# Cross-attention beside self-attention cells: where the weights are divided by their sum, how far their transposes follow the scores, and the number of places for parts

## The chip, the cores and the metric

The kernel runs on one core of a Trainium2 chip. The metric is the device time of one execution in microseconds (us); less is better. A core has five engines that run their own instruction streams in order and wait for one another through semaphores: TensorE (PE, matrix products; its weight loads are listed as PEld), VectorE (DVE), ScalarE (ACT), GpSimd (POOL) and SyncE (SP, which issues most of the DMA transfers). Tiles lie in SBUF; PE writes its results to the eight banks of PSUM, each 128 partitions by 512 float32 numbers.

## The reference

A chain of two transformer blocks over x of 2 batches x 1024 tokens x 256 features, all in float32. Each block has self-attention (16 heads of 16 features, 1024 keys), cross-attention to a context of 64 rows per batch, and a feed-forward part. In block 0 the feed-forward part is a mixture: a router picks two of eight experts for each token. In block 1 it is one dense network, and the cross-attention's scores get a bias of -10000 where the mask is 0. Cut to the cross-attention, which is what the change touches:

```python
def layer_norm(x, w, b):
    mu = jnp.mean(x, axis=-1, keepdims=True)
    var = jnp.mean(jnp.square(x - mu), axis=-1, keepdims=True)
    return (x - mu) * jax.lax.rsqrt(var + EPS) * w + b
...
xn = layer_norm(x, ln1_w, ln1_b)
q = _heads(xn @ q_w.T)                  # 16 heads of 16
k = _heads(codebook_embeds @ k_w.T)     # 64 keys per batch
v = _heads(codebook_embeds @ v_w.T)
attn = jnp.einsum('bhnd,bhmd->bhnm', q, k) * SCALE
bias = (1.0 - codebook_mask.astype(attn.dtype))[:, None, None, :] * -10000.0
attn = jax.nn.softmax(attn + bias, axis=-1)
ca = _merge(jnp.einsum('bhnm,bhmd->bhnd', attn, v)) @ ca_proj_w.T
x = x + ca
```

Block 0 does the same without the bias, with biases on the projections.

## The kernel before

**One order for four engines.** The whole program is one function, and the order of the instructions on PE, DVE, ACT and SP is the order in which the Python code issues them; only POOL's is left to a scheduler. Around the change this order comes from two things: a loop over cells, and a stream of tasks that fills the cells.

**Cells.** Self-attention of a block is cut into 16 passes (2 batches x 2 halves of the queries x 4 groups of four heads), each of 8 cells (blocks of 128 keys), so 128 cells per block; `for cell in range(ncell + 2)` (L959) runs over them. A cell has, in this order on PE: four score matmuls with keys on partitions (`score` of kind "b", L816), interleaved with four score matmuls for the cell ten ahead (kind "a", L805; `LEAD = 10`), from which DVE takes row maxima out of PSUM (L812); ACT takes exponentials of the four "b" banks into SBUF (L822). Every second cell `product` (L858) multiplies the exponentials of two cells by the values (L867, eight matmuls into one bank). Its first result of a pass is copied by ACT to `acc` (L876), each later one to a tile `part` (L879), which is then added to `acc` (L880). Two places are allotted for `part`. The addition is on the engine that `helper()` names: POOL as long as maxima are still to be taken (`maxima[0]`), DVE in the last ten cells of a block. A cell that has only this is called bare.

**The stream.** Everything else of a block is cut into tasks, Python generators that issue some instructions and then yield: a positive number is the declared cost of what was issued, a number of zero or below is a wait, which puts the task's next step at least one cell later, and more cells for a longer wait (in units of `CELL = 2.9`). In every cell the loop takes steps from the tasks that are able to run until their declared cost reaches a rate, 2.5 a cell in block 0 and 1.1 in block 1 (more where tasks have a due cell). What is left when the cells are over is run behind them by `Stream.rest`, in the order of rank; that stretch is called the tail of a block. A bank is taken from the list `free` and put back when the code that drains it has been issued, so a later user of the bank waits on chip for the one that drains it.

**Cross-attention.** It is worked in four units a block, each of 512 queries (`cross_tasks`, L1076, in both blocks). A unit is three tasks one behind the other: `norm` (layer norm and transposes to features on partitions), `weigh` (L1103) and `share` (L1273, the output projection, L437 and L445). A unit starts its norm when the one before it is "weighed". `weigh` makes the queries q_c (L1113, L1120) and then works in two groups g of eight heads; a group has four tiles r of two heads each, 128 queries on partitions by 4 blocks of queries x 2 heads x 64 keys:

- scores of two tiles (L1143; in block 1 the mask's bias is put into the bank by matmuls first, L1134), copied by ACT to sc_c in SBUF (L1154);
- `largest`: a maximum over the 64 keys on DVE (L1163), subtracted by POOL in place (L1164); in the tail both are on DVE and read PSUM;
- `weights_turned`: four 128x128 transposes per tile on PE (L1179), then the exponential on ACT from PSUM to pt_c (L1183);
- `product`: four matmuls by the values (L1192), copied by ACT over q_c (L1209); and the sums of the exponentials by 16 matmuls with columns of ones and zeros out of `picks` (L1202), whose reciprocals DVE takes as one 128x128 tile (L1211);
- `divided`: four matmuls spread the reciprocals over the heads' rows (L1217), and DVE multiplies q_c by them (L1224). For the second group this stands at the start of `share`.

A unit that begins while maxima are being taken follows a list of 11 steps, mostly one step a cell; in the tail it follows another list of the same steps with shorter waits.

**Mixture, block 0.** Behind each unit's `share` stands its dispatch (`dispatch_task`, L1306): router (L1332), ranks by a matmul (L1392), and the scattering of the rows to their experts by POOL's indirect DMAs (L1429). The experts' tiles (`expert_tiles`, L1442) load sorted rows through SP (L1570), transpose them (L1622) and run the two layers of each expert (L1656, L1686). Block 1's feed-forward part is `forward_task` (L1816, L1828).

**Other users of what the change touches.** `side_by_side` (L756 to L782) closes the last self-attention heads of block 0 and has a reciprocal tile `inv` of its own. `picks` is a constant of 768 columns loaded once; O_SUM, O_HEAD, O_ROWS and O_PART are the column offsets of its parts. The tag "xn" has six places of 128x256 for centred rows (L357) in the pool `small`.

## Time and profile before

| what | us |
|---|---|
| three runs | 1624.6, 1626.58, 1629.66; median 1626.58 |
| the profiled execution | 1611.58 |
| its span, first to last instruction | 1609.8 |
| mean granted TensorE clock in it | 0.988 |

The same execution by stretches, cut at whole microseconds near the first score of a cell (busy time of each engine, us, as the profile's windows give it):

| stretch | length | PE | DVE | ACT | POOL | clock |
|---|---|---|---|---|---|---|
| 0 to 52, before the first cells | 52 | 42.0 | 34.2 | 14.3 | 16.0 | 0.97 |
| 52 to 254, cells 0 to 51 of block 0 | 202 | 200.6 | 150.5 | 145.4 | 64.3 | 0.95 |
| 254 to 583, cells 52 to 127 with cross-attention | 329 | 323.8 | 240.3 | 224.0 | 109.8 | 0.98 |
| 583 to 943, tail of block 0 | 360 | 354.3 | 147.2 | 125.4 | 68.1 | 1.00 |
| 943 to 1175, cells 0 to 60 of block 1 | 232 | 229.7 | 170.3 | 170.3 | 67.5 | 1.00 |
| 1175 to 1446, cells 61 to 127 with cross-attention | 271 | 266.6 | 192.6 | 188.7 | 74.4 | 1.00 |
| 1446 to 1610, tail of block 1 | 164 | 157.9 | 47.6 | 46.7 | 10.9 | 1.00 |

How to read the profile's lines: a group of instructions gives its line in the kernel, its engine, the operation, what is written and read by the tiles' names, partitions x elements, how many there are, then busy time in us and the mean ns of one, then the idle time of the engine just before them and what ended most of it. Matmuls are pipelined, so the time of one matmul from start to end is longer than the distance from its start to the start of the one behind it; the busy time of a group of matmuls counts such overlaps once. A line of the timeline gives the start, the duration, the engine and the line, and in brackets the wait ahead of it and who ended it.

### The profile page before, as it was taken

Reading aid. Unit: us, or ns where it says so; the run is one execution under the profiler, and the core shown is the slowest. Engines: PE = TensorE matmul, PEld = TensorE weight load, DVE = VectorE, ACT = ScalarE, POOL = GpSimd, SP = SyncE. Lnnn points to the kernel's source line nnn. Section 1 sums busy time; section 2 is a strip of 40 time slices with the busy share of each in tenths; the row PEclk is TensorE's granted clock in tenths of the full one; section 3 lists DMA queues with packets and bytes.
Section 4 is the critical chain, followed back from the end, with each engine's and each line's share of the span. In section 5 each row is a group of like instructions: output and inputs, shape, how many; then the busy total and the mean of one; then the engine's idle time right before and its main releaser. Section 6 shows DMA issues by size and latency. Waiting matters only on the chain. (4 is left out here: it accounts for less than half of the span.)

```text
span 1609.8 us, 28322 instructions
## 1 busy us (share of the span) xinstructions
PE 1574.8 (98%) x10710; PEld 876.0 (54%) x10710; DVE 982.6 (61%) x2094; ACT 914.7 (57%) x1770; POOL 410.9 (26%) x546
## 2 busy tenths in 40 slices
PE   7999999999999999999999999999999999999998
PEld 3433444444544447888888653344344445446766
DVE  5797766677679747511114458876777777854400
ACT  3487767666765665332223337876776676674321
POOL 2233423135235203311112033411222322311000
PEclk9899999999999999999999999999999999999999
DMA  5334311101000115386556320101010002000000
GB/s 158 114 134 169 138 27 31 28 25 47 15 21 34 54 50 196 105 278 205 187 188 216 92 78 23 35 21 24 31 38 17 22 14 84 20 9 21 14 13 26
DMA packets 55751, 121.07 MB, mean 75 GB/s; under 512 B 12218, under 2 KB 26428, under 8 KB 55228
## 3 DMA queue, kind: packets, MB, share of 16 engines
q1 hardware_dynamic: 51772, 109.07, 20.9%
q0 software_dynamic: 3456, 9.51, 1.6%
q8 instruction: 86, 1.41, 0.4%
q10 hardware_dynamic: 384, 0.66, 0.2%
q14 instruction: 53, 0.43, 0.1%
HBM read 71.68 MB, written 38.88 MB: 69 GB/s over the span
## 5 line engine op out<-in xcount | busy, mean ns | idle before, releaser
L812 DVE TENSOR_REDUCE mx_s<-banks 128x1 f32<-128x512 f32 x1024 | 634.0, 681 | 209.5 <-PE banks L805 207.2
L822 ACT ACTIVATE pt_s<-banks 128x512 f32<-128x512 f32 x1024 | 532.8, 609 | 157.1 <-PE banks L805 123.8
L805 PE MATMUL banks<-KS,QS 16*128 16x512 f32 x2048 | 535.1, 631 | 2.9 <-DVE count L1446 1.4
L816 PE MATMUL banks<-qb_s,KS 32*128 32x512 f32 x2048 | 516.8, 622 | 6.9 <-DVE qb_s L715 3.6
L880 POOL TENSOR_TENSOR acc_s<-acc_s,part_s 128x512 f32<-128x512 f32 x141 | 179.4, 1272 | 434.5 <-ACT part_s L879 433.9
L816 PEld LDWEIGHTS banks<-qb_s,KS 32*128 32x128 f32 x2048 | 180.8, 187 | 178.7 <-DVE mx_s L812 106.3
L867 PE MATMUL banks<-pt_s,v_s 128*20 128x512 f32 x2048 | 262.7, 604 | 1.5 <-DVE mx_s L812 1.0
L805 PEld LDWEIGHTS banks<-KS,QS 16*128 16x128 f32 x2048 | 200.3, 186 | 71.7 <-issue 34.2
L867 PEld LDWEIGHTS banks<-pt_s,v_s 128*20 128x20 f32 x2048 | 43.1, 98 | 185.8 <-ACT pt_s L822 130.4
L1686 PE MATMUL banks<-w_slot,h_s 128*128 128x256 f32 x640 | 143.1, 380 | 0.0
L1686 PEld LDWEIGHTS banks<-w_slot,h_s 128*128 128x128 f32 x640 | 120.6, 190 | 19.7 <-DVE mx_s L812 1.5
L879 ACT COPY part_s<-banks 128x512 f32<-128x512 f32 x155 | 92.7, 598 | 62.3 <-PE banks L867 52.6
L1695 DVE SCALAR_TENSOR_TENSOR ys<-banks,gate,b 128x256 f32<-128x256 f32 x40 | 19.3, 482 | 163.0 <-PE banks L1686 161.8
L1662 ACT ACTIVATE h_s<-banks,w_slot 128x256 f32<-128x256 f32 x104 | 43.7, 471 | 111.1 <-issue 64.0
L1656 PE MATMUL banks<-xsT,w_slot 128*128 128x256 f32 x416 | 95.4, 381 | 0.7 <-ACT xsT L376 0.7
L1701 POOL DMA_INDIRECT results<-ys,to x40 | 38.8, 970 | 223.0 <-DVE ys L1695 180.5
L1656 PEld LDWEIGHTS banks<-xsT,w_slot 128*128 128x128 f32 x416 | 77.4, 190 | 14.9 <-DVE mx_s L812 2.3
L1164 POOL TENSOR_TENSOR sc_c<-sc_c,mx_c 128x512 f32<-128x512 f32 x38 | 40.0, 1053 | 97.6 <-DVE mx_c L1163 97.5
L1819 ACT ACTIVATE h_f<-banks,w_ff 128x512 f32<-128x512 f32 x32 | 22.0, 687 | 73.9 <-PE banks L1816 73.9
L635 PE MATMUL banks<-xT_s,w_att 128*128 128x512 f32 x128 | 63.9, 635 | 0.0
L1828 PE MATMUL banks<-w_ff,h_f 128*128 128x256 f32 x256 | 57.3, 380 | 0.0
L1662 ACT ACTIVATE h_s<-banks,spare 128x256 f32<-128x256 f32 x56 | 23.4, 471 | 58.7 <-issue 30.4
(272 smaller groups left out, 1640.2 us busy)
## 6 DMA issues: line engine op xcount, KB each, us to landing
w_slot<-in_ff_w_dram SPq DMA_DIRECT2D x40, 576.0 KB
sorted_rows<-fill SPq DMA_DIRECT2D x36, 520.0 KB
w_slot<-in_ff_w_dram SPq DMA_DIRECT2D x26, 514.0 KB
whole<-acc_s SPq DMA_DIRECT2D x30, 256.0 KB
spare<-in_ff_w_dram SPq DMA_DIRECT2D x14, 514.0 KB
xs<-sorted_rows SPq DMA_DIRECT2D x20, 260.0 KB
y<-results SPq DMA_DIRECT2D x16, 256.0 KB
QS<-stq_s SPq DMA_DIRECT2D x124, 32.0 KB
```

What stands on the lines that cost most here:

```text
L635: nc.tensor.matmul(p, lhsT=w[:, at + k * D + pair * P : at + k * D + (pair + 1) * P], rhs=xT[b][:, k, blk * 512 : (blk + 1) * 512], start= ...
L805: nc.tensor.matmul(sc, lhsT=QS[h % 4][r, qc * P : (qc + 1) * P], rhs=K[r, kh * 512 : (kh + 1) * 512], start=True, stop=True,)
L812: return i, lambda: nc.vector.tensor_reduce(mx[h][:, qc, j, kh : kh + 1], sc, AX.X, ALU.max)
L816: nc.tensor.matmul(sc, lhsT=K[r, n * P : (n + 1) * P], rhs=QB[h][r, :], start=True, stop=True)
L822: nc.scalar.activation(pt, sc, AF.Exp, scale=SCALE)
L867: nc.tensor.matmul(o[32 * j : 32 * j + VW, :], lhsT=V[b][:, cell % 8, 4 * g + j, :], rhs=exps.pop((cell, j)), start=(cell == cells[0]), st ...
L879: nc.scalar.copy(part, o)
L880: helper().tensor_tensor(acc[h], acc[h], part, ALU.add)
L1656: nc.tensor.matmul(ph[:, n, :], lhsT=w[:, at : at + P], rhs=xT[:, k, :], start=(k == 0), stop=(k == 1),)
L1662: nc.scalar.activation(h1[:, f, :], ph[:, n, :], AF.Gelu, bias=w[:, W_B1 + f : W_B1 + f + 1])
L1686: nc.tensor.matmul(py, lhsT=h1[:, f, h * P : (h + 1) * P], rhs=w[:, f * D : (f + 1) * D], start=(f == 0), stop=(f == 7),)
L1828: nc.tensor.matmul(py[:, n, :], lhsT=h1[:, f, t * P : (t + 1) * P], rhs=w2[:, f * D : (f + 1) * D], start=(f == 0), stop=(f == 7),)
```

## The change

For units that begin while maxima are being taken (`whole`), the weights are now finished with queries on partitions, ahead of the transposes:

- after the subtraction ACT takes the exponential in SBUF in place (`exponentials`), DVE sums over the 64 keys and takes the reciprocals of the eight sums per partition, and `helper()` multiplies the tile by them (`divided`);
- `weights_turned` then transposes finished weights, and ACT only copies them out of PSUM;
- `product` has only the four matmuls by the values and ACT's copy; the sums by matmul, the spreading of reciprocals and the multiplication of q_c are left out, in `share` too.

Such a unit follows a schedule over 19 cells: tile k (0 to 7) has its scores and its subtraction in cell k + 4g (scores for two tiles together), the exponential two cells later, sum and division three cells later; the transposes of two tiles stand seven cells behind their scores, and the products of the groups in cells 11 and 18. Between the cells of this schedule the task yields 0.0 while maxima are being taken and -1.5 afterwards.

A unit that begins in the tail keeps the old steps, renamed `undivided` and `division`, with the masks of ones read from 32 columns that are shifted by 2r in place of four sets of 32. Three further edits: `picks` shrinks from 768 to 680 columns, with its parts moved; the tiles of reciprocals lie in the "xn" places and not in tags of their own; and `part` has three places instead of two.

```diff
@@ -104,10 +104,11 @@
 NCOL = 139
 
 
-O_SUM, O_HEAD = 0, 128
-O_ROWS, O_PART = 640, 704
-NPICK = 768
+O_SUM, O_HEAD = 512, 0
+O_ROWS, O_PART = 552, 616
+NPICK = 680
 
 W_O, W_V, W_Q, W_K = 0, 512, 1024, 1536
 NSELF = 2048
@@ -766,7 +767,7 @@
                         start=(half == 0),
                         stop=(half == 1),
                     )
-            inv = small.tile([P, P], F32, tag="inv", name=f"inv_{names}", bufs=1)
+            inv = small.tile([P, D], F32, tag="xn", name=f"inv_{names}", bufs=6)[:, :P]
             nc.vector.reciprocal(inv, s[:, :P])
             nc.scalar.copy(dst, o)
             free.extend((j, i))
@@ -875,7 +876,7 @@
                 acc[h] = opool.tile([P, 512], F32, tag="acc", name=f"acc_{names}{h}")
                 nc.scalar.copy(acc[h], o)
             else:
-                part = opool.tile([P, 512], F32, tag="part", name=f"part_{names}{cells[0]}")
+                part = opool.tile([P, 512], F32, tag="part", name=f"part_{names}{cells[0]}", bufs=3)
                 nc.scalar.copy(part, o)
                 helper().tensor_tensor(acc[h], acc[h], part, ALU.add)
             free.append(n)
@@ -1125,11 +1126,15 @@
         shape = [P, 4 * 2, SK]
         less, pts, whole_scores = {}, {}, set()
 
+        whole = maxima[0]
         def scores(g, n):
 
             got = [(r, *bank()) for r in (2 * n, 2 * n + 1)]
+            masked = layer == 1
             for t in range(4):
-                for r, _, p in got if layer == 1 else ():
+                for r, _, p in got if masked else ():
                     at = slice(32 * r, 32 * r + 1)
                     nc.tensor.matmul(
                         p[:, t * P : (t + 1) * P].rearrange("p (u k) -> p u k", k=SK),
@@ -1144,7 +1149,7 @@
                         p[:, t * P : (t + 1) * P],
                         lhsT=q[rows, g, t * P : (t + 1) * P],
                         rhs=kbd[rows, g, b].rearrange("p u k -> p (u k)"),
-                        start=(layer == 0),
+                        start=not masked,
                         stop=True,
                     )
             for r, i, p in got:
@@ -1169,6 +1174,17 @@
         def largest(g, r):
             if (g, r) in whole_scores:
                 subtract(less[g, r], less[g, r], nc.gpsimd, f"{g}{r}")
+        def exponentials(g, r):
+            nc.scalar.activation(less[g, r], less[g, r], AF.Exp, scale=SCALE)
+        def divided(g, r):
+            sc = less[g, r].rearrange("p (c k) -> p c k", k=SK)
+            sm = pool.tile([P, 8], F32, tag="smc", name=f"sm_{name}{g}{r}", bufs=4)
+            nc.vector.tensor_reduce(sm, sc, AX.X, ALU.add)
+            nc.vector.reciprocal(sm, sm)
+            helper().tensor_tensor(sc, sc, sm.unsqueeze(2).to_broadcast(shape), ALU.mult)
 
         def weights_turned(g, n):
 
@@ -1180,13 +1196,14 @@
                         p[:, t * P : (t + 1) * P], sc[:, t * P : (t + 1) * P], ident
                     )
                 pt = pts[g, r] = pool.tile([P, 512], F32, tag="p1", name=f"pt_{name}{g}{r}", bufs=4)
-                nc.scalar.activation(pt, p, AF.Exp, scale=SCALE)
+                if whole:
+                    nc.scalar.copy(pt, p)
+                else:
+                    nc.scalar.activation(pt, p, AF.Exp, scale=SCALE)
                 free.append(i)
 
-        inverse = {}
         def product(g):
             i, o = bank()
             for r in range(4):
                 nc.tensor.matmul(
@@ -1196,22 +1213,37 @@
                     start=True,
                     stop=True,
                 )
+            nc.scalar.copy(q[:, g, :], o)
+            free.append(i)
+        inverse = {}
+        def undivided(g):
+            i, o = bank()
+            for r in range(4):
+                nc.tensor.matmul(
+                    o[32 * r : 32 * (r + 1), :],
+                    lhsT=vbd[:, b, 4 * g + r, :],
+                    rhs=pts[g, r],
+                    start=True,
+                    stop=True,
+                )
             j, s = bank()
             for r in range(4):
                 for c in range(4):
                     nc.tensor.matmul(
                         s[32 * c : 32 * (c + 1), :P],
-                        lhsT=picks[:, O_SUM + 32 * r : O_SUM + 32 * (r + 1)],
+                        lhsT=picks[:, O_SUM + 6 - 2 * r : O_SUM + 38 - 2 * r],
                         rhs=pts[g, r][:, c * P : (c + 1) * P],
                         start=(r == 0),
                         stop=(r == 3),
                     )
             nc.scalar.copy(q[:, g, :], o)
-            inv = inverse[g] = pool.tile([P, P], F32, tag="inv", name=f"inv_{name}{g}", bufs=2)
+            inv = inverse[g] = small.tile([P, D], F32, tag="xn", name=f"inv_{name}{g}", bufs=6)[:, :P]
             nc.vector.reciprocal(inv, s[:, :P])
             free.extend((i, j))
 
-        def divided(g):
+        def division(g):
             i, p = bank()
             for c in range(4):
                 nc.tensor.matmul(
@@ -1224,33 +1256,36 @@
             nc.vector.tensor_tensor(q[:, g, :], q[:, g, :], p, ALU.mult)
             free.append(i)
 
-        held.update(ot=q, divided=divided)
-        cost = 1.9 if layer else 1.0
-        SC, LA, TU, PR, DI = scores, largest, weights_turned, product, divided
-        if maxima[0]:
-            for now, wait in (
-                (((SC, 0, 0), (LA, 0, 0)), 0.0),
-                (((LA, 0, 1),), 0.0),
-                (((SC, 0, 1), (LA, 0, 2)), 0.0),
-                (((TU, 0, 0), (LA, 0, 3)), 0.0),
-                (((SC, 1, 0), (LA, 1, 0)), 0.0),
-                (((TU, 0, 1), (LA, 1, 1)), 0.0),
-                (((SC, 1, 1), (LA, 1, 2)), 0.0),
-                (((PR, 0), (LA, 1, 3)), -1.5),
-                (((TU, 1, 0),), None),
-                (((DI, 0), (TU, 1, 1)), -1.4),
-                (((PR, 1),), None),
-            ):
+        held.update(ot=q, division=None if whole else division)
+        costs = {
+            scores: 1.9 if layer else 1.0, weights_turned: 1.15, product: 0.55,
+            undivided: 1.1, division: 0.55,
+        }
+        SC, LA, EX, DI, TU, PR = (
+            scores, largest, exponentials, divided, weights_turned, product
+        )
+        if whole:
+            cells = [[] for _ in range(19)]
+            for k in range(8):
+                g, r = divmod(k, 4)
+                at = k + 4 * g
+                if r % 2 == 0:
+                    cells[at].append((SC, g, r // 2))
+                    cells[at + 7].append((TU, g, r // 2))
+                cells[at].append((LA, g, r))
+                cells[at + 2].append((EX, g, r))
+                cells[at + 3].append((DI, g, r))
+            for g in range(2):
+                cells[11 + 7 * g].append((PR, g))
+            for now in cells:
                 for step, *args in now:
                     step(*args)
-                us = sum({SC: cost, TU: 1.15, PR: 1.1, DI: 0.55}.get(step[0], 0.0) for step in now)
+                us = sum(costs.get(step, 0.0) for step, *_ in now)
                 if us:
                     yield us
-                if maxima[0]:
-                    yield 0.0
-                elif wait is not None:
-                    yield wait
+                if now is not cells[-1]:
+                    yield 0.0 if maxima[0] else -1.5
             return
         for step, *args, wait in (
             (SC, 0, 0, None),
@@ -1258,23 +1293,24 @@
             (TU, 0, 0, None),
             (SC, 1, 0, None),
             (TU, 0, 1, -1.3),
-            (PR, 0, None),
+            (undivided, 0, None),
             (SC, 1, 1, None),
             (TU, 1, 0, None),
-            (DI, 0, None),
+            (division, 0, None),
             (TU, 1, 1, -1.6),
-            (PR, 1, None),
+            (undivided, 1, None),
         ):
             step(*args)
-            yield {SC: cost, TU: 1.15, PR: 1.1, DI: 0.55}[step]
+            yield costs[step]
             if wait:
                 yield wait
 
     def share(w, name, first, held):
 
-        yield -2.6
-        held["divided"](1)
-        yield 0.55
+        if held["division"]:
+            yield -2.6
+            held["division"](1)
+            yield 0.55
         yield -1.2
         for t0 in range(0, 4, 2):
             yield from project_task(held["ot"], w, first + t0, t0, 2)
@@ -2095,10 +2131,9 @@
     cols[:E, C_RB] = l0["router_b"]
 
     picks = np.zeros((P, NPICK), f32)
-    for r in range(4):
-        for u in range(2):
-            for c in range(4):
-                picks[SK * u : SK * (u + 1), O_SUM + 32 * r + 8 * c + 2 * r + u] = 1.0
+    for u in range(2):
+        for c in range(4):
+            picks[SK * u : SK * (u + 1), O_SUM + 6 + 8 * c + u] = 1.0
     for j in range(4):
         for d in range(DH):
             picks[32 * j + d, O_ROWS + DH * j + d] = 1.0
```

## What the change is predicted to do

> **What bounds the kernel now.** I read the busy shares first, then the timeline of a cell that carries nothing but attention, then the groups of cross-attention by line, and the waits last.
>
> ```profile
> span 1609.8 us, 28322 instructions
> PE 1574.8 (98%) x10710; PEld 876.0 (54%) x10710; DVE 982.6 (61%) x2094; ACT 914.7 (57%) x1770; POOL 410.9 (26%) x546
> ```
>
> PE is never long idle, but the shares are a mean over stages. The next lines are one bare cell of block 0 (its first score at 187.93, the next cell's at 190.87, so 2.92 to 2.94 us; cells 34 to 37 all take that).
>
> ```profile
> 187.93 0.70 PE L816 MATMUL banks<-qb_s,KS 32*128 32x512 f32 x2
> ...
> 189.09 2.06 ACT L822 ACTIVATE pt_s<-banks 128x512 f32<-128x512 f32 x4 [0.31 <-PE banks L805]
> 189.18 2.48 DVE L812 TENSOR_REDUCE mx_s<-banks 128x1 f32<-128x512 f32 x4 [0.43 <-PE banks L805]
> ...
> 189.88 1.05 PE L867 MATMUL banks<-pt_s,v_s 128*20 128x512 f32 x8
> ...
> 190.87 0.70 PE L816 MATMUL banks<-qb_s,KS 32*128 32x512 f32 x2
> ```
>
> Four maxima take 2.48 us together, so one follows another after 0.60 (2.48 = 3 x 0.60 + 0.68); four exponentials take 2.06, 0.48 apart. DVE needs 4 x 0.60 = 2.4 and ACT, with the part's copy, 5 x 0.48 = 2.4 of the 2.92; both then wait for PE (0.31 and 0.43 in the brackets). On PE a pass of 512 columns follows the last after 0.43 (the product's two passes start at 189.88 and 190.32): six passes are 2.57, and 0.35 goes where row groups change to column groups and back. So a bare cell is PE's, with half a microsecond to spare on DVE and ACT: less than one 128x512 instruction of theirs (0.60 and 0.48). That margin is the whole question.
>
> ```profile
> L1217 PE MATMUL banks<-inv_c,picks 128*128 128x128 f32 x128 | 17.6, 280 | 0.3 <-DVE inv_c L1211 0.2 <-DVE mx_s L812 0.2
> L1202 PE MATMUL banks<-pt_c,picks 128*32 128x128 f32 x512 | 17.5, 273 | 0.0
> L1164 POOL TENSOR_TENSOR sc_c<-sc_c,mx_c 128x512 f32<-128x512 f32 x38 | 40.0, 1053 | 97.6 <-DVE mx_c L1163 97.5
> L1183 ACT ACTIVATE pt_c<-banks 128x512 f32<-128x512 f32 x64 | 35.6, 612 | 20.6 <-PE banks L1179 19.9 <-ACT pt_c L1183 0.6
> L1163 DVE TENSOR_REDUCE mx_c<-sc_c 128x8 f32<-128x512 f32 x38 | 25.6, 673 | 14.7 <-ACT sc_c L1154 14.7
> L1211 DVE RECIPROCAL inv_c<-banks 128x128 f32<-128x128 f32 x16 | 15.3, 958 | 25.3 <-PE banks L1202 25.3
> L1224 DVE TENSOR_TENSOR q_c<-q_c,banks 128x512 f32<-128x512 f32 x16 | 10.9, 682 | 12.8 <-PE banks L1217 12.8
> ```
>
> The first two are what the change takes from PE, over 16 groups (eight units of two): matmuls that follow one another with no idle time before them.
>
> **Part 1, what leaves PE.** The changed kernel's order of instructions shows five units beside cells (units 0, 1, 2 of block 0; 0, 1 of block 1), so ten groups: 40 of the 128x128 matmuls and 160 of the 32x128 ones go. A 128-column pass takes 0.107 us, a quarter of the 0.43. A group of L1217 is 8 passes (0.85 us), a group of L1202 is 32 passes, four at a time (0.85). So 10 x 1.7 = 17.1 us. Transposes and products stay.
>
> **Part 2, what the other engines get.** DVE: 40 sums at 0.673 (row L1163, also from SBUF) = 26.9; 40 reciprocals of 128x8, whose bounds are 0.133 (128x2, L422) and 0.338 (128x32, L497) and which I take at 0.18 as the 128x4 of L1409, = 7.1; ten multiplications that fall past the last maxima, at 0.685, = 6.9; four additions of parts, 2.8; less 10 x (0.958 + 0.682) = 16.4: +27 us. ACT: 40 exponentials from SBUF; no row has that, the bounds are 0.598 (copy, L879) and 0.687 (L1120), I take 0.61 as L1183: 24.4; the old 40 become copies at no change; 13 more copies of parts, 7.8; two fewer copies of scores, 1.2: +31. POOL: 30 multiplications at 1.05, nine additions at 1.27, two subtractions fewer: +41. [...]
>
> **Part 3, whether that fits beside the cells.** From the order I counted each cell's instructions on PE, DVE and ACT, and took as its floor the largest of: PE's passes + 0.35; DVE's durations x 0.9 (0.60 / 0.681); ACT's x 0.8 (0.48 / 0.61). Cell 65 of block 0 as an example: before, PE has 3.41 + 0.35 = 3.76 against DVE's 3.41 x 0.9 = 3.1, floor 3.76; after, PE has 2.92, DVE four maxima, a sum and two small ones, 3.57 x 0.9 = 3.2, floor 3.2: of 0.85 us saved on PE 0.55 is kept.
>
> | cells | measured | floors before | floors after | PE before | PE after |
> |---|---|---|---|---|---|
> | block 0, 52 to 126 | 329.1 | 313.3 | 299.3 | 264.4 | 248.2 |
> | block 1, 61 to 126 | 270.3 | 263.0 | 247.2 | 228.3 | 210.8 |
>
> Measured is from the first score of the first cell to that of the cell behind (254.35 to 583.48; 1175.33 to 1445.64). The floors of before are 5 and 3% low, so I trust their differences: -14.0 and -15.8. Cells led by DVE rise from 40 to 49 of 141, by ACT from 15 to 24.
>
> **Part 4, what moves behind the cells.** A unit now lasts 19 cells where it took 11 steps, so unit 2 of both blocks ends later. The order has 5.9 us more PE work behind the cells of block 0 and 10.6 behind those of block 1 (there the whole of unit 2). Both tails are PE's, so it counts in full: +16.5. In block 0 the dispatch of unit 2 now runs together with unit 3's scores, and the next experts' rows wait for it:
>
> ```profile
> 613.64 1.00 POOL L1429 DMA_INDIRECT sorted_rows<-xd_m,at_m  x1 [24.60 <-DVE mine_m L1418]
> ...
> 622.55 0.96 POOL L1429 DMA_INDIRECT sorted_rows<-xd_m,at_m  x1 [0.30 <-issue]
> ```
>
> From the rank matmul L1392 (606.83) to the first scatter is 6.8, to the last 15.7, and SP's load of rows waits until 629.3 for it to land; some 25 us, against 26.6 of PE work between L1392 and the rows' transposes before and 18.1 after. Before, that stretch took 31.9, so 5.3 idle; after, at least 7 idle. I take +4 (0 to +10). Block 1's tail: unit 2 beside a feed-forward block, +1.5 (0 to +5).
>
> **Part 5, edits costed at nothing.** The third place for parts removes a wait of ACT on POOL that is 6.9 us in three places (bounds -7 and 0); POOL's 41 us more use it up. Inverses in the centred tiles' six places: only the last units still make them, 0 to +1. The narrower table of picks lands hundreds of microseconds before its first use. Waits: EX stands in ACT's queue ahead of the next cell's four exponentials and waits for POOL's subtraction of two cells ago; the sum stands ahead of four maxima and waits for EX of one cell ago. POOL has at most 1.27 + 2 x 1.05 = 3.4 us in a cell, once a group, and the multiplication has four cells until its transpose. Beside a dispatch (cells 84 to 88) it has 4 x 1.27 + 6 x 1.05 + 8 scatters at 1.27 = 21.5 against floors of 21.6: just enough. SP's queue issues the same transfers.
>
> [...]
>
> ```profile
> 514.31 2.20 DVE L357 TENSOR_SCALAR xn_c<-x_sb,mv_c,rs_c 128x256 f32<-128x256 f32 x2
> 515.07 1.28 POOL L880 TENSOR_TENSOR acc_s<-acc_s,part_s 128x512 f32<-128x512 f32 x1
> ```
>
> Two centrings, 0.40 each elsewhere, take 2.20 while POOL adds. The 38 reductions of L1163, beside a busy POOL too, have a mean of 673 ns and a maximum of 687, so I charge the sums nothing. [...]
>
> **Sum.** -14.0 - 15.8 + 16.5 + 4 + 1.5 = -8 us. The profiled execution took 1611.58 (span 1609.8), so 1603.8; the runs shown have a median of 1626.58, 15 us more, and the same difference gives 1618.5.
>
> **Rivals.** A, full gain: the waits in parts 3 and 4 are hidden and all of PE's 17 us is kept: 1609.5. For it: PE leads 86 of the 141 cells before. Against: the margin is below one instruction. B, slower: DVE and ACT take the cells over, because a sum or EX late in its in-order queue holds back the maxima and exponentials behind it, and with them PE's banks. Place: the cells with a subtraction and a sum and no other PE work; point: 4 x 0.60 + 0.60 + 0.75 = 3.75 against 2.92. If DVE's 27 us are paid in full against 17 saved: +10, 1636.5. It takes 0.19 us more per cell than my floors, (10 + 8) over 95 cells. For it: 106.3 us of PE's weight loads already end on DVE's maxima. C, no change: the gain in the cells is given back behind them (part 4 at +12 instead of +5.5): 1625. That fewer units take the new path is excluded: the order shows 40 sums.
>
> **Chances.** 0.3% (4.9 us) is about what a measurement of this kernel tells from no change. Forecast (1614 to 1621) 0.32, A 0.15, C 0.20, B 0.33. So faster 0.47, the same 0.20, slower 0.33. The range, 1606 to 1637, holds A and B up to their middles and somewhat beyond, with part 4's bounds; the forecast's own is 1611 to 1621.
>
> **What would show it.** Right: rows of PE for the sums and the spread inverses fall to six groups; the cells 52 to 126 of block 0 take about 315 us, 61 to 126 of block 1 about 255; the tails grow by 10 and 12. Wrong: more idle time of PE before L816 and L867 released by DVE and ACT (B); a stall before the transposes of xs behind block 0's cells (C); a stretch of half clock other than that at 518 to 528, which is worth 5 us by itself.

## The result, and the profile after

The changed kernel takes 1626.29 us (median of 20 runs, 1623.62 to 1629.41) against 1626.54 for the kernel before on the same chip (20 runs, 1623.37 to 1631.01): a ratio of 0.9998, 95% interval 0.9989 to 1.0006. That is no change. Two later comparisons of the same two kernels gave 0.9975 (0.9964 to 0.9986) and 0.9989 (0.9973 to 1.0005), so by these 2 to 4 us may be gained. (The ratios here and below are the record's comparison of the runs, each with its 95% interval; they differ from the quotient of the two medians by up to 0.0015.) The kernel before has a median of 1613.7 us on one of the chips used here and of 1627.8 to 1628.9 on the three others of the later runs; times are compared only between runs on one chip.

The head of the page of the changed kernel, first profiled execution (1624.14 us):

```profile
span 1622.4 us, 27769 instructions
...
PE 1568.8 (97%) x10310; PEld 861.8 (53%) x10310; DVE 1017.7 (63%) x2184; ACT 940.6 (58%) x1823; POOL 446.2 (28%) x569
```

Its groups by line, each shape apart, show that the instructions are those that were counted. The sums and the spread inverses on PE (now L1234 and L1249) are left for six groups, and the new steps stand in their place:

```profile
L1187 POOL TENSOR_TENSOR sc_c<-sc_c,sm_c 128x512 f32<-128x512 f32 x30 | 31.3, 1045 | 14.0 <-DVE sm_c L1186 10.9 <-DMA QS<-stq_s 3.1
L1185 DVE TENSOR_REDUCE sm_c<-sc_c 128x8 f32<-128x512 f32 x40 | 26.9, 672 | 0.0
L1179 ACT ACTIVATE sc_c<-sc_c 128x512 f32<-128x512 f32 x40 | 26.2, 655 | 0.0
L1234 PE MATMUL banks<-pt_c,picks 128*32 128x128 f32 x192 | 8.4, 281 | 3.2 <-issue 3.2
L1186 DVE RECIPROCAL sm_c<-sm_c 128x8 f32<-128x8 f32 x40 | 8.1, 203 | 1.4
L1249 PE MATMUL banks<-inv_c,picks 128*128 128x128 f32 x48 | 6.3, 275 | 0.0
```

The durations are near those assumed: the sum 0.672 (0.673), the reciprocal 0.203 (0.18), the multiplication on POOL 1.045 (1.05), the exponential out of SBUF 0.655 (0.61, so 26.2 us and not 24.4).

Where the time went is read from windows over the stretches, cut at the first score of cells 0, 52 and 127 of block 0 and of cells 0, 61 and 127 of block 1. Both kernels were profiled again on one chip for this. The columns are the length, the busy time of PE, PEld, DVE, ACT and POOL with their instructions, the granted clock, the DMA share and GB/s. The kernel before (span 1622.9):

```profile
50.31:251.20 200.89, 199.44 (x1379) 81.86 (x1377) 150.28 (x270) 145.20 (x283) 64.21 (x86) 0.96 0.30 103
251.20:586.59 335.39, 329.11 (x2523) 153.43 (x2523) 240.30 (x483) 224.81 (x433) 109.76 (x141) 0.97 0.10 29
586.59:954.06 367.47, 355.41 (x1830) 288.46 (x1829) 147.65 (x523) 124.66 (x268) 67.70 (x71) 0.99 0.50 167
954.06:1186.72 232.66, 230.29 (x1640) 93.55 (x1641) 170.61 (x299) 170.28 (x323) 67.76 (x79) 1.00 0.13 36
1186.72:1457.06 270.34, 265.92 (x2278) 127.51 (x2275) 192.38 (x342) 188.73 (x364) 74.40 (x108) 1.00 0.10 30
1457.06:1622.90 165.84, 159.90 (x908) 110.70 (x904) 47.65 (x99) 46.73 (x74) 10.94 (x32) 0.99 0.06 18
```

The changed kernel (span 1617.3):

```profile
49.99:247.19 197.20, 197.07 (x1379) 82.01 (x1377) 150.20 (x270) 144.94 (x283) 64.23 (x86) 0.97 0.30 105
247.19:561.56 314.37, 306.03 (x2243) 133.65 (x2242) 255.09 (x514) 232.41 (x451) 129.07 (x160) 0.97 0.10 31
561.56:946.01 384.45, 366.20 (x1869) 296.02 (x1868) 154.74 (x535) 126.31 (x273) 68.43 (x71) 0.98 0.47 160
946.01:1178.51 232.50, 229.99 (x1641) 93.44 (x1641) 170.93 (x299) 170.04 (x323) 67.72 (x79) 1.00 0.13 36
1178.51:1433.36 254.85, 252.08 (x1996) 114.56 (x1992) 192.57 (x344) 195.43 (x379) 85.05 (x96) 1.00 0.10 31
1433.36:1617.30 183.94, 175.78 (x1025) 120.75 (x1024) 61.19 (x143) 57.66 (x89) 16.55 (x48) 0.98 0.05 17
```

Line by line: -3.7, -21.0, +17.0, -0.2, -15.5, +18.1, and -0.3 ahead of the first cell: -5.6, the difference of the two spans. The cells with cross-attention gain 36.5 us, and the two tails give 35.1 of it back. The chip of the result's own comparison has no trace of the kernel before, so the split there isn't known; the first trace of the changed kernel has tails of 387.5 and 184.7.

The tail of block 0 of the kernel before, by what TensorE waited for longest (who waits, for whom, us in total, times, longest):

```profile
PE banks L1143 <- ACT q_c L1120: 3.0, 1, 3.0
PE banks L1686 <- ACT h_s L1662: 2.9, 1, 2.9
PE banks L756 <- DVE acc_s L880: 2.1, 1, 2.1
```

The same view of the changed kernel:

```profile
PE banks L370 <- DVE xd_m L1355: 6.0, 1, 6.0
PE banks L370 <- DVE xn_c L358: 3.6, 2, 1.9
PE banks L370 <- DMA ctx<-in_ctx_dram: 2.1, 1, 2.1
PE banks L1249 <- issue: 1.5, 1, 1.5
PE banks L1428 <- DVE chosen_m L1408: 1.2, 1, 1.2
```

What stalls now is unit 3: the transposes of its norm (xn_c) and of its dispatch's norm (xd_m) wait for VectorE. Unit 3's norm starts when unit 2 is weighed, and unit 2 now ends behind the cells. The forecast stall, before the transposes of xs, is 0.4 us here; with the new path in block 0 alone (below) it is 3.2 us, beside 1.7 for xd_m.

### The profile page after: what moved, and what is told of

The parts are those of the page before. It is cut to its first block, busy times and chain, and to the rows that moved or that the text cites. A ratio compares the mean times of both kernels' runs of the same rounds, so it can differ in the third digit from the quotient of the medians.

```text
span 1622.4 us, 27769 instructions
## 1 busy us (share of the span) xinstructions
PE 1568.8 (97%) x10310; PEld 861.8 (53%) x10310; DVE 1017.7 (63%) x2184; ACT 940.6 (58%) x1823; POOL 446.2 (28%) x569
## 5 line engine op out<-in xcount | busy, mean ns | idle before, releaser
L881 POOL TENSOR_TENSOR acc_s<-acc_s,part_s 128x512 f32<-128x512 f32 x150 | 190.3, 1269 | 361.9 <-ACT part_s L880 360.8
L868 PE MATMUL banks<-pt_s,v_s 128*20 128x512 f32 x2048 | 267.6, 604 | 2.7 <-DVE mx_s L813 1.9
L1722 PEld LDWEIGHTS banks<-w_slot,h_s 128*128 128x128 f32 x640 | 121.6, 192 | 20.5 <-DVE mx_s L813 1.5
L880 ACT COPY part_s<-banks 128x512 f32<-128x512 f32 x168 | 102.7, 611 | 44.9 <-PE banks L868 40.7
L1692 PEld LDWEIGHTS banks<-xsT,w_slot 128*128 128x128 f32 x416 | 78.5, 193 | 15.6 <-DVE mx_s L813 2.3
L1852 PE MATMUL banks<-hT_f,w_ff 128*128 128x512 f32 x128 | 57.2, 595 | 0.0
```

The source lines that it names most:

```text
L868: nc.tensor.matmul(o[32 * j : 32 * j + VW, :], lhsT=V[b][:, cell % 8, 4 * g + j, :], rhs=exps.pop((cell, j)), start=(cell == cells[0]), st ...
L880: nc.scalar.copy(part, o)
L881: helper().tensor_tensor(acc[h], acc[h], part, ALU.add)
L1692: nc.tensor.matmul(ph[:, n, :], lhsT=w[:, at : at + P], rhs=xT[:, k, :], start=(k == 0), stop=(k == 1),)
L1722: nc.tensor.matmul(py, lhsT=h1[:, f, h * P : (h + 1) * P], rhs=w[:, f * D : (f + 1) * D], start=(f == 0), stop=(f == 7),)
L1852: nc.tensor.matmul(ph, lhsT=w1[:, at : at + P], rhs=hT[:, k, :], start=(k == 0), stop=(k == 1))
```

## The experiments

Fifteen runs, in groups by what they tell apart. The diffs are against the changed kernel; where several "+" lines stand for one "-" line, they are those of the kernels told below it, in that order.

**The kernel before again, and the places alone.** The first is the kernel before as it is.

> The kernel before, unchanged, profiled a second time: what an ordinary execution of it looks like, since its profiled one took 1611.58 us and its runs have a median of 1626.5. Theory of the tails: the cells take what they took (block 0, cells 52 to 126: about 329; block 1, cells 61 to 126: about 270) and the difference of some 13 us lies in half-clock stretches of TensorE, wherever they fall (more than the 37.5 us of half clock of the first trace). Rival, a lasting difference: the tail of block 0 takes 370 or more here and not 359, at the same clock, so that the tails of the change lose less than they seem to.

It took 1615.98 us (span 1614.2), beside a median of 1613.68 for 17 runs of the kernel before on that chip. Cells and tails are those of the first trace to 1.1 us (330.2, 358.7, 270.4, 164.2); half clock (stretches in which the granted clock is 0.5, without the one at the very end) is 41.0 us and not 37.5. The rival's 370 isn't seen on this chip; a later trace on another shows 367.5.

In the second, no unit takes the new path, and the list of the 11 steps beside cells is back, with `undivided` and `division`:

```diff
-        whole = maxima[0]
+        whole = maxima[0] and False
...
+        if maxima[0] and not whole:
...
```

> The changed kernel with no unit on the new path: the old steps everywhere, three places for parts, narrower picks and inverses in the centred tiles' places. The order of the instructions is that of before. Theory: three places take away at most the 6.9 us of idle time that ACT spent on POOL's additions, of which little was on the path, so -2 to 0 us (1624 to 1627). Rival: the places are what gains in the cells and the division is what loses: -5 us or more.

1606.85 against 1613.68: ratio 0.9947 (0.9932 to 0.9962). More than expected, and in one place: the first 52 cells take 197.1 (202.2 and 203.4 in the traces of before), every other stretch is within 2 us. So the rival's "-5 us or more" for the places came true. This is what the first cells lose in the kernel before (timeline of its trace on the last chip, the idle time ahead of each in brackets with who ended it):

```profile
133.66 1.26 POOL L508 TENSOR_TENSOR ot_s<-ot_s,by_s 128x512 f32<-128x512 f32 x1 [7.46 <-DMA by_s<-turns]
134.89 2.60 POOL L880 TENSOR_TENSOR acc_s<-acc_s,part_s 128x512 f32<-128x512 f32 x2
136.18 0.59 ACT L879 COPY part_s<-banks 128x512 f32<-128x512 f32 x1 [3.14 <-POOL acc_s L880]
136.82 0.70 PE L805 MATMUL banks<-KS,QS 16*128 16x512 f32 x2 [1.45 <-ACT part_s L879]
```

POOL divides a finished pass (L508), two additions queue behind it and hold both places; ScalarE waits 3.14 us for one, and TensorE 1.45 for ScalarE. Behind that stall lies a stretch of half clock (137.7 to 141.1 here, 6.8 us long in the two other traces of before). With a third place both are gone. That it is the third place, and not the other two edits, is shown by the run with two places below.

**Which block, which unit.** The condition on `whole` is narrowed, and units that fail it have the 11 old steps.

```diff
-        whole = maxima[0]
+        whole = maxima[0] and layer == 0
+        whole = maxima[0] and name not in ("c02", "c11")
+        whole = maxima[0] and name in ("c00", "c01")
```

> The new path for units beside cells in block 0 alone; block 1 has its old steps. Theory of the tails: the cells 52 to 126 of block 0 take about 314 (-15), its tail some 15 to 25 more than before's, so 1620 to 1637 in all, the tail with stalls of TensorE before the transposes of xd_m, xn_c and the context. Rival, the clock: the tail has no more idle time than before and the loss is half clock, in any part of the span.

1613.06, ratio 1.0003 (0.9989 to 1.0017), on the same chip as the places alone: 6.2 us above them, so in block 0 as a whole the new path in all three units loses. Cells of block 0 316.2, its tail 378.2 (358.7 in the trace of before on this chip), with the stalls named. Half clock in the tail is only 6.8 us, so the rival explains a small part.

> The new path for units 0 and 1 of block 0 and unit 0 of block 1; the last unit that begins beside cells in each block (unit 2 of block 0, unit 1 of block 1) has the 11 old steps and so ends 7 to 9 cells sooner. Theory of the tails: two thirds of the cells' gain in block 0 and half of it in block 1 stay (-10 and -8), and the tails are as before's, so 1605 to 1615 us. Rival, that the loss isn't made by the last unit's delay but by DVE and ACT work or by the clock: 1622 to 1630.

1601.08, ratio 0.9910 (0.9893 to 0.9927). Block 0: cells 320.6, tail 359.4, as before's. So the tail's loss there is made by unit 2, and the kernel is 5.8 us below the places alone. Block 1 did not follow: cells -7, but its tail took 175.3 and not 164. Of these 11 us half clock is about 5 (10.7 us of it, none before). For the rest, unit 0's 19 cells make the two units behind it late even where these have the old steps: unit 2's first product starts 14.0 us behind the first score of the last cell, and 4.9 in the kernel before.

> The new path for units 0 and 1 of block 0 alone; all else with the old steps. Theory of the tails: block 0's cells 52 to 126 keep 8 to 9 us, its tail is as before's (359), the stall in the first cells is gone (-5), block 1 is as before's (270 and 164): 14 to 19 us below before, and 2 to 5 below the kernel with the new path in unit 0 of block 1 too. Rival: without block 1's 7 us in the cells it is slower than that one.

1608.57 against 1628.85: ratio 0.9874 (0.9855 to 0.9893), 20 us below before on this chip. The ratio is lower than the last one's by 3.6 per mille, but that one is from another chip; by their traces block 1 takes 4.1 us less. Cells of block 0 320.7, block 1 as before (270.4 and 164.2). The tail of block 0 took 370.3 on this chip, with two stalls of 3 us on ScalarE; the kernel before has the same two on the last chip (367.5).

**Lateness in block 1.** The stream's rate is raised so that units begin sooner.

```diff
-RATE = (2.5, 1.1)
+RATE = (2.5, 1.5)
-        whole = maxima[0]
+        whole = maxima[0] and name != "c02"
+        whole = maxima[0] and name in ("c00", "c01")
```

> Units 0 and 1 of block 0 and units 0 and 1 of block 1 on the new path, with the stream's rate in block 1 at 1.5 instead of 1.1, so that units begin sooner there and unit 2 of block 1 stands in the cells again, as before the change. Theory of the tails (the new path itself gains; only its lateness costs): block 1's cells take about 270 less 7 plus the moved work, 263 to 268, its tail falls to 164 or less; together 4 to 8 us below the sum of before's (434.5). Rival, the path itself costs more in block 1 than the 6.8 us of TensorE that it removes (ScalarE's and VectorE's margins): the sum stays at 434 or above.

1604.56, ratio 0.9858 (0.9839 to 0.9877): the lowest ratio of the study, though its interval overlaps that of the kernel above. Block 1 takes 238.4 + 272.9 + 153.4 = 664.7, the changed kernel on this chip 232.5 + 254.9 + 184.2 = 671.6, units01 667.2. Cells 61 to 127 and the tail are 8.2 us below the 434.5 of the expectation, but the cells ahead of them are 5.8 longer than in the kernel above, so 2.5 us are left. Against the changed kernel 3 of the 6.9 us are half clock (1.9 us against 8.4). So the new path, begun sooner, gains in block 1, but by a few us.

> The control to the one with the higher rate: the same rate of 1.5 in block 1, with the old steps there. Theory of the tails: a higher rate by itself moves work from the tail into the cells at about the same price, so within 4 us of the kernel with units 0 and 1 of block 0 alone; the kernel with the new path in block 1 at this rate is 3 to 7 us below this. Rival: at this rate the old steps are as fast or faster, the new path has no gain in block 1.

1617.9, ratio 0.9934 (0.9920 to 0.9949), 13 us above the kernel with the new path at this rate: more than either theory said. Its block 1 takes 679.4, of which 24.6 us are at half clock (1.9 in the other); the clock's part, half of the difference of 22.7, is 11 of the 14.7 us, so what is left for the path is 3 to 4.

**The seven cells.** The same work with shorter distances.

```diff
-            cells = [[] for _ in range(19)]
+            cells = [[] for _ in range(16)]
-                at = k + 4 * g
+                at = k + 2 * g
-                    cells[at + 7].append((TU, g, r // 2))
+                    cells[at + 5].append((TU, g, r // 2))
-                cells[11 + 7 * g].append((PR, g))
+                cells[9 + 6 * g].append((PR, g))
```

> The change in all five units, but with transposes five cells behind their scores and not seven, and the second group 6 cells behind the first instead of 8, so that a unit lasts 16 cells and not 19. The work is the same. In the order, unit 2 of block 0 then ends within the cells. Theory of the tails (lateness costs, not the path): the cells of block 0 take 317 to 321 (a little more work inside), its tail 360 to 372 instead of 378 to 388; block 1's tail 175 to 182 instead of 184; 10 to 20 us below the change as it stands, ratio to before 0.985 to 0.992. Rival, POOL and ScalarE need the seven cells: the transposes wait for multiplications, the cells take 325 or more and the total is no better than the change's (0.997 to 1.003).

1622.22, ratio 0.9960 (0.9943 to 0.9978). Both theories hold in part: the tails fall to 371.7 and 167.6, and the cells of both blocks rise to 326.8 and 268.9. TensorE waited 9.3 us for POOL's multiplications in the cells of block 0, 6.3 of it at once, beside a dispatch (timeline of POOL, then TensorE):

```profile
398.92 1.04 POOL L1169 TENSOR_TENSOR sc_c<-sc_c,mx_c 128x512 f32<-128x512 f32 x1
400.12 1.00 POOL L1465 DMA_INDIRECT sorted_rows<-xd_m,at_m  x1 [0.17 <-issue]
401.43 0.97 POOL L1465 DMA_INDIRECT sorted_rows<-xd_m,at_m  x1 [0.31 <-issue]
402.42 1.27 POOL L881 TENSOR_TENSOR acc_s<-acc_s,part_s 128x512 f32<-128x512 f32 x1
403.64 1.04 POOL L1187 TENSOR_TENSOR sc_c<-sc_c,sm_c 128x512 f32<-128x512 f32 x1
```

```profile
404.73 0.69 PE L1195 MATMUL banks<-ident,sc_c 128*128 128x128 f32 x2 [6.29 <-POOL sc_c L1187]
```

The scatters stand ahead of the multiplication in POOL's queue. With seven cells between scores and transposes the changed kernel's trace has no wait of TensorE for POOL's multiplications.

> Units 0 and 1 of both blocks on the new path with the short schedule of 16 cells, unit 2 of block 0 with the old steps, rate 1.5 in block 1. Theory of the tails: like the same kernel with 19 cells (ratio 0.986) or up to 4 us better, since units in block 1 end sooner and unit 2 there begins sooner. Rival (the short delay costs waits): 3 to 10 us worse than that.

1628.76, ratio 1.0002 (0.9984 to 1.0021): the rival, and worse than it said. Its trace is of one of its longest executions (1635.09): cells 327.4 and 283.6, the second with 30.7 us of half clock. A schedule that waits for POOL is not saved by an earlier start.

**VectorE's margin.**

```diff
-            helper().tensor_tensor(sc, sc, sm.unsqueeze(2).to_broadcast(shape), ALU.mult)
+            nc.vector.tensor_tensor(sc, sc, sm.unsqueeze(2).to_broadcast(shape), ALU.mult)
```

> The change, with all multiplications by the reciprocals on DVE and none on POOL: 30 instructions of some 0.69 us move to DVE (+20.5 us) and 30 of 1.05 us leave POOL (-31.5). Theory that DVE has little to spare in the cells (a margin below one instruction in a bare cell): the two stretches of cells with cross-attention take 4 to 10 us more, ratio to the change 1.003 to 1.006. [...]

1636.05, ratio 1.0054 (1.0034 to 1.0073). Cells 321.1 and 264.2; with 314.0 to 316.4 and 254.9 in the changed kernel that is 14 to 16 us, more than the 4 to 10 of the theory, for 24 us of work put on VectorE. But the trace is of the longest of its seven executions, 6 us above the median; by the medians on this chip (1629.95 for the next kernel, which also loses 3.7 us in the first cells) it is some 10 us. The multiplications on VectorE, first in the changed kernel and then here:

```profile
L1187 DVE TENSOR_TENSOR sc_c<-sc_c,sm_c 128x512 f32<-128x512 f32 x10 | 7.1, 711 | 0.3
L1187 DVE TENSOR_TENSOR sc_c<-sc_c,sm_c 128x512 f32<-128x512 f32 x40 | 31.5, 787 | 1.4
```

(31.5 less the 7.1 that it had.) So VectorE has little time to spare there. The forty also show that this multiplication (sc_c by sm_c) can be stretched beside POOL: the 23 that overlap no instruction of POOL take 0.69 each, and the 17 that do take 0.69 to 2.22.

**Two places in the changed kernel.**

```diff
-                part = opool.tile([P, 512], F32, tag="part", name=f"part_{names}{cells[0]}", bufs=3)
+                part = opool.tile([P, 512], F32, tag="part", name=f"part_{names}{cells[0]}")
```

> The change with two places for parts, as before it. Theory: the stall of TensorE in the first cells of block 0 (1.6 us and a half-clock stretch behind it, 5.4 us together) is back, and POOL's load of 30 more multiplications makes one to three such stalls more between cells 52 and 126: ratio to before 1.000 to 1.006, the first 52 cells 202, the stretch with cross-attention 316 to 322. Rival: the third place has no use once the division is on the new path: 0.997 to 0.999, like the change.

1629.95, ratio 1.0016 (1.0001 to 1.0031). The stall of 1.5 us in the first cells is back (200.7 and not 197.0); the cells with cross-attention are the same (314.0 and 254.5). So the third place is worth its 4 to 6 us (3.7 on the last chip, 6.3 on the first) in one spot, and isn't used up by POOL's new work.

**The sum on one chip, and lateness alone.** The changed kernel was run twice more; the second time there are also a trace of the kernel before on the same chip and the old steps with a delay:

> The changed kernel, unchanged, beside the same runs of before as the next three. Theory of the tails: the same as before again (ratio 0.998 to 1.002), block 0's tail about 380 (between 378.2 and 387.4), block 1's 180 or more, and the stalls of TensorE at the same places as in its first trace; the half-clock stretches behind them may be others. Rival, chance: 1% faster or slower than before on this chip, with tails of 365 and 168.

1624.63, ratio 0.9975 (0.9964 to 0.9986); tails 388.6 and 184.2, stalls as in the first trace.

> The kernel before, unchanged, for a trace from the same chip as the next two. If this is a chip on which it takes some 1627 us and not 1613: theory that the difference between chips lies in the tail of block 0 and in half clock: its tail 366 to 371 there (359 elsewhere), with one or two stalls of about 3 us of TensorE on ScalarE, and more than 40 us of half clock; the cells as elsewhere to 2 us. Rival: the cells of before take 5 us or more longer on such a chip, so that the change's gain in the cells is larger there.

1624.64. Its tail of block 0 is 367.5, with two stalls of 3 us on ScalarE; half clock 44.4 us. Its cells of block 0 took 335.4 and not 329 to 330, so there the rival was right too.

> The changed kernel beside it. Theory of the tails, part by part against before on the same chip: first 52 cells -5, cells of block 0 with cross-attention -13 to -15, tail of block 0 +17 to +20, cells of block 1 -15.5, its tail +20; ratio 0.997 to 1.001. Rival: the parts don't add up to the ratio within 3 us, and something in before that isn't in these parts is missing.

1623.59 against 1627.79: ratio 0.9989 (0.9973 to 1.0005). The parts, shown above, add up to the difference of the spans; the gain in block 0's cells was larger than expected.

```diff
+        if name == "c02":
+            for _ in range(9):
+                yield 0.0
         shape = [P, 4 * 2, SK]
```

(and `whole` is false throughout)

> The old steps everywhere, with the places of the change, and nine cells of waiting put ahead of the scores of unit 2 of block 0: lateness alone, without any work of the new path. Theory of the tails: the tail of block 0 grows by 12 to 20 us as with the new path, the cells lose the work that moves out of them (-4 to -8); ratio to before 1.000 to 1.006, against 0.995 for the same kernel without the delay. Rival: the tail's loss comes from the new path's instructions (its exponentials and multiplications behind the cells), and lateness alone costs 3 us at most: 0.994 to 0.997.

1631.13, ratio 1.0024 (1.0009 to 1.0038). The tail of block 0 took 373.6, 6.1 more than before on the same chip: between the two theories. The cells of block 0 did not lose 4 to 8 us but took 3.3 more (338.7 against 335.4), with 27.3 us of half clock against 17.1. Nine cells of waiting made unit 2 later by less than was meant. The table counts, in the traces, from the first score of the last cell to the rank matmul of unit 2's dispatch; the idle time is TensorE's in the tail, its length less the time in which TensorE is busy. Kernels are to be compared on one chip.

| chip | kernel | ranks of unit 2 | tail of block 0 | idle | half clock |
|---|---|---|---|---|---|
| first | before | +23.0 | 358.7 | 6.2 | 0 |
| first | new path in block 0 | +51.9 | 378.2 | 15.6 | 6.8 |
| second | unit 2 with old steps (units 0 and 1 of block 0 new) | +22.9 | 370.3 | 11.6 | 13.7 |
| second | changed kernel | +52.3 | 388.6 | 21.5 | 20.5 |
| third | unit 2 with old steps (the other new units on 16 cells, rate 1.5 in block 1) | +22.8 | 370.4 | 11.6 | 13.7 |
| third | new path over 16 cells | +33.8 | 371.7 | 11.1 | 10.2 |
| last | before | +23.3 | 367.5 | 12.1 | 6.8 |
| last | old steps delayed | +33.9 | 373.6 | 12.1 | 10.2 |
| last | changed kernel | +50.1 | 384.5 | 18.3 | 13.7 |

Unit 2 on 19 cells ends 27 to 29 us later, and on three chips the tail is 17 to 19.5 longer, with 6 to 10 us more idle time. Some 11 us late cost 1.3 and 6.1, with no more idle time, whether the steps are new (16 cells) or old (delayed). So the stalls come with the long schedule of unit 2 and not with the new instructions as such. That lateness alone makes them is not shown: no kernel has the old steps 27 us late.

## Why the prediction was wrong

The measured 1626.29 lies inside the range and 7.8 us above the forecast of 1618.5, next to rival C's 1625: the forecast said faster, and it is the same.

**What held.** The bound (a bare cell is TensorE's, with less than one instruction to spare on VectorE and ScalarE) agrees with the multiplications on VectorE: of 24 us of added work 10 to 16 were paid. Part 3, the cells: block 1 was to give -15.8 and gave -15.5; block 0 was to give -14.0 and gave -21.0 on the last chip, but -14 (330.2 to 316.2) where the kernel with the new path in block 0 ran. Part 2's work on VectorE, ScalarE and POOL fits beside the cells. Rival B, those two taking the cells over, is excluded by these stretches. Part 5's count of POOL beside a dispatch (21.5 against 21.6, "just enough") is what the shorter schedule shows from the other side. Part 5 charged the sums nothing for POOL's work beside them, and that held for the reciprocals too: in the changed kernel's trace 22 of the 40 reciprocals have POOL beside them for more than half of their time and 17 not at all, and both take 0.203; the same split of the 40 sums, 17 and 17, takes 0.672 and 0.676. (Of the 38 reductions that the prediction took for this, only nine overlap an instruction of POOL.) The multiplications on VectorE did pay, in the run that had all forty there: 0.69 to 2.22 us beside POOL against 0.69.

**The step that failed is part 4.** It took +4 (0 to +10) for stalls in block 0's tail and +1.5 (0 to +5) in block 1's, beside 5.9 and 10.6 of moved work. Measured on the last chip are +17.0 and +18.1, so 11.1 and 7.5 beyond that work: both above the upper bound. By the windows above, TensorE's idle time (length less busy time) is 6.2 of the 11.1 and 2.2 of the 7.5, 8.4 together, more than the forecast 5.5 but within its bounds. What the sum had at nothing is the half clock in the tails: 13.7 us against 6.8 in block 0 and 8.6 against 3.8 in block 1, at half speed an estimated 3.4 and 2.4. The rest, 1.5 and 2.9, is time in which TensorE is busy, beyond the moved work that was counted; why stays open.

Part 4 also misread the trace of before. It took 5.3 idle us out of the 31.9 between the rank matmul and the rows' transposes, as the length less the time of the passes. By the profile's window of 607 to 639 TensorE is busy there for 30.63 of 32.00 us, so 1.4 are idle.

The stall was looked for in one place, at the rows of unit 2 (xs), and priced by what stands between. The chain does not end there: unit 3's norm, scores and dispatch stand behind unit 2 in the same order, and by the order each now runs later, with less of TensorE's other work beside it. The largest stall shows it (timeline of the changed kernel, VectorE and then TensorE):

```profile
643.99 0.94 DVE L332 TENSOR_TENSOR root_m<-rs_m 128x4 f32<-128x4 f32 x1
644.96 0.16 DVE L333 TENSOR_TENSOR root_m<-root_m,root_m 128x4 f32<-128x4 f32 x1
...
649.94 0.16 DVE L1681 TENSOR_TENSOR gate<-gate,xs 128x2 f32<-128x2 f32 x1
650.32 1.38 DVE L1355 TENSOR_SCALAR xd_m<-x_sb,mv_m,rs_m 128x256 f32<-128x256 f32 x4 [0.21 <-issue]
...
650.79 1.12 PE L370 MATMUL banks<-ident,xd_m 128*128 128x128 f32 x4 [5.95 <-DVE xd_m L1355]
```

A chain of small instructions on VectorE, a few of them stretched from 0.16 to 0.94 while POOL fills tiles (its copies of 1.03 us run beside them), and the index arithmetic of two experts' tiles queued ahead of xd_m: TensorE, whose order puts these transposes next, waits 6 us for it. With the new path in block 0 alone, on the first chip, this wait is 1.7 us, so its size depends on more than the lateness.

**A smaller miss** in part 5: the third place was put at nothing, because POOL's new work would use it up. It is worth 3.7 to 6.3 us, because the stall sits in cells without cross-attention, where POOL has no new work, and because half clock follows it (3.4 and 6.8 us long in the traces of before).

**So** rival C came true ("the gain in the cells is given back behind them (part 4 at +12 instead of +5.5)"): on the last chip that term is +18.6, though its stall before xs is only 0.4 us. The larger gains elsewhere (7 in block 0's cells, on a chip where these take 5 us longer before, and 3.7 from the third place) took up the rest. That the sum came out no further off is luck in part: a term above its bound met gains that were not forecast.

## What to carry to other kernels

When work is spread over more cells to hide its waits, look at where its last step lands as well as at its instructions. Here a unit that ended some 11 us later cost the tail 1 to 6 us and no stall; one that ended 27 to 29 us later cost 17 to 19.5, with stalls of the unit chained behind it. Put the long schedule where the end has room, keep the short one for the last unit, or start sooner: kernels arranged that way were 0.7 to 1.4% faster than before, of which the edits to the places alone give 0.5%. Price a stall with the half clock that can follow it (mostly 3.4 to 10.2 us long here). Between a step on a busy in-order queue and its reader, count the longest foreign run in that queue: a run with eight scatters was covered here by seven cells and not by five.

## What the runs showed of the hardware

In these traces half clock mostly follows idle time of TensorE, but not every idle piece is followed by it. In the 17 traces of this study, from 70 us behind the start to the last 5 us, 91 stretches of half clock lie; 70 of them begin within 6 us of an idle piece of TensorE (no matmul running) of 1 us or more. Of idle pieces of 1.5 us or more 42 of 76 were followed by one within 7 us, of 1.0 to 1.5 us 34 of 76, of 0.55 to 1.0 us 18 of 190. The traces share most of their code, so these are not independent cases. All but three of the stretches last 3.4, 6.8 or 10.2 us. In them TensorE's passes of the product by the values start 0.81 to 0.83 us apart and not 0.42 (first trace of the kernel before, 518 to 528 and 187 to 194), so by an estimate, half of 10.2, a stall of 1.5 us can cost up to 5 us more. The kernel before has 37.5, 41.0 and 44.4 us of it in its three traces. Its runs have a mean granted clock of 0.987 to 0.988 on the chip where it takes 1613.7 us and of 0.983 on those of 1628; (0.017 x 1628) - (0.0125 x 1614) gives an estimate of 7.5 of the 14 us between them.
